# The head of a fused convolution, scan and attention kernel: order of the weights, depth of the convolution's pipeline, places for two buffers

## The chip, the cores and the metric

The kernel runs on one core of a Trainium2 chip. The core has a matrix engine (TensorE, PE in the profile), a vector engine (VectorE, DVE), a scalar engine (ScalarE, ACT), a general engine (GpSimd, POOL) and SyncE (SP), which here only issues transfers. Each runs its own list of instructions in order and waits on semaphores for the others. The metric is the time of one execution on the device in microseconds (us); lower is better.

## The reference, cut to what matters

The input `x` is (4, 64, 64, 96): four images. Layer 0 is a binarised Mamba-like block with four scan directions, layer 1 a linear attention and a quantised feed-forward. What bears on this case is the start of layer 0:

```python
xz = bilinear(x, W_in, s_in, b_in)            # sign(x) @ (s * sign(W - mean(W))).T + b
xp, z = jnp.split(xz, 2, axis=-1)             # 192 channels each
t = bq_quad(xc + move0_b)                     # the sign of xp, as channels by 64x64
t = conv3x3(t, mean|conv_W| * sign(conv_W))   # 192 -> 192 channels
t = prelu(t + conv_b + rp_b0) + rp_b1 + xc
xconv = jax.nn.silu(t)                        # called u in the kernel
x_hwwh = jnp.stack([x_flat, x_tr], axis=1)    # by rows and by columns
xs = jnp.concatenate([x_hwwh, jnp.flip(x_hwwh, axis=-1)], axis=1)   # four directions
x_dbl = bilinear(xin, Wl, sl, bl)             # per direction: 6 dt rows, 16 B, 16 C
dts = bilinear(dts_r, Wd, sd, bd)             # -> 192 step sizes per position
# selective scan over 4096 positions, 192 channels x 16 states, for each direction:
#   h = exp(dt * A) * h + dt * u * B;   y = sum(h * C) + D * u
# then LayerNorm, gate with silu(z), output projection, and layer 1
```

## The kernel before

The scans of the four images are one long loop of 1536 pieces (image, direction, chunk of 1024 positions, group of 32 channels, quarter of the states), which needs in each piece one product on POOL, one exponential on ACT, one scan on DVE, and a product on DVE or POOL. What the images need ahead of their scans (the prologue) runs beside the scans of the image before. Only the first image has nothing to run beside: its prologue is the **head** of the program. There the prologue (`first`, with `alone` true) and the preparation of all weights (`made`) are two generators; each `yield` hands over to the other, so the order of instructions on each engine is the order in which they take turns.

```python
made, first = c.weights(), prologue(c, 0, c.xts)
lanes = [made, first]
next(made)
for _ in range(6):
    next(first)
while (0, 1) not in c.ready:
    interleave(lanes)          # one step of each
    c.later.tick()
assert made not in lanes
scans = Scans(c)
```

`c.later` holds stores back: `store(dst, src, after=2)` is issued on SP's queue two ticks later, so that SP, which runs in order, need not wait for the data.

The prologue transposes the image (`xps`), takes its signs (`xsT`) and a copy with bias (`xb`), projects it (`ix`, `iz`: PSUM tags `y0` and `y1`; their signs `tp` and `sz` by ACT), and runs the convolution in 16 parts of 96 channels by 512 positions:

```python
for n, part in enumerate(parts + [None]):
    if part:
        h, q = part
        ps = c.p.dA.tile([128, CH], F32, ...)[0:96, 0:512]      # alone
    for s in range(4 if alone else 5):
        # four of the 15 taps of this part:  matmul(ps, w, tp)
        if alone and ahead:                     # project ahead, 12 parts of 16
            if s == 0:
                next(ahead[0])                  # matmuls ix, iz
            elif s == 2:
                next(ahead.pop(0), None)        # ACT: tp, sz
        if prev:                                # the part before
            ph, pq, pz, v, r, pn = prev
            if s == 0:                          # alone
                c.vec.scalar_tensor_tensor(pz, pz, S_X, v, ALU.mult, ALU.add)
                c.vec.scalar_tensor_tensor(pz, r, oma, pz, ALU.mult, ALU.add)
            elif s == 1:
                sign(ph, pq, pz)                # ACT sg, three stores into xg
                nc.scalar.activation(e, pz, AF.Exp, scale=-1.0)
            elif s == 2:
                nc.scalar.activation(e, e, AF.Ln, bias=1.0)
                nc.scalar.activation(e, e, AF.Exp, scale=-1.0)
            elif s == 3:
                c.vec.tensor_tensor(u, pz, e, ALU.mult)
                c.later.store(c.ud[b][ph][...], u)
                by_columns(ph, pq, u)           # POOL copies u turned into ut; utd <- ut
        yield
    if part:
        nc.vector.tensor_scalar(v, ps, acs, acb, ALU.mult, ALU.add)
        nc.scalar.activation(r, ps, AF.Relu, scale=csc, bias=cbias)
        pz = bank("cz" + nm, n % 2)
        nc.tensor.matmul(pz, winT, xsT)
        prev = (h, q, pz, v, r, nm)
        yield
```

(Cut: the branches for the other images, and arguments.) `sg`, `e`, `u`, `v`, `r`, `xb` are tiles of pool `f`, which has 8 buffers taken in turn. `ut` has a pool of its own, beside the convolution's tiles; the pool of the rows, opened next, takes over that memory.

The rows stage turns `xg` into rows (`xr`, twelve copies by ACT and DVE in turn), multiplies with the weights of two directions (`acc`), and writes B, C (`tbc`, stored to `bcd`) and the signs for dt (`sgn`, stored to `sgd`), in two halves. Each of `xa`, `xb`, `acc` is a PSUM bank of two in turn: `bank(f"xa{o}{n}", n % 2)`. `sgd` comes back as `g` and is turned into `gT`.

Then `Scans.start` loads the first columns of u and the first B (`bc`), computes the first step sizes, and sends them through a copying transfer to the scan's tiles (`dl_s`):

```python
w = [p.w.tile([128, CH], F32, name=f"w_s{x}", tag="w") for x in range(8)]
t, d2, us = w[4:6], w[6], w[2:4]
nc.sync.dma_start(v[0], ud[0:128, 0:16])                 # us, from utd
for q in range(NQ):
    self.load_bc(0, self.bt, 0, 0, 0, q)                 # four of 512 KB
for x in range(2):
    nc.sync.dma_start(v[1][64 * x : 64 * x + 64, 0:8], ud[128:DN, 8 * x : 8 * x + 8])
...
r = p.dl.tile([128, CH], F32, name=f"dl{x}_s{n}", tag=f"dl{x}")
nc.sync.dma_start(r, w[x][32 * n : 32 * n + 32].unsqueeze(1).to_broadcast([32, 4, CH]))
```

Of the kernel before, what the change touches and what calls it, by code (L numbers as in the profile page):

```python
# [25 lines left out]
CH = 1024  # L26
# [27 lines left out]
def hybrid_kernel(ctx: ExitStack, tc: tile.TileContext, a: dict, out: bass.AP):  # L54
# [108 lines left out]
    def weights():  # L163
# [110 lines left out]
        part = temp("part", [96, 2, 2])  # L274
        for i, cut in enumerate(cuts):
            nc.scalar.activation(cwA.rearrange("p t d -> p (t d)")[:, cut], cfa[i], AF.Sign, saturate=False)
            nc.scalar.activation(cwB[:, lines[i]], cfb[i], AF.Sign, saturate=False)
            for h in range(2):
                nc.vector.tensor_reduce(part[:, h, i : i + 1], cwn[h][i], AX.X, ALU.add, apply_absolute_value=True)
        nc.vector.tensor_tensor(csc, part[:, :, 0], part[:, :, 1], ALU.add)  # L280
        nc.vector.tensor_scalar(csc, csc, 1.0 / (9 * DN), None, ALU.mult)
        yield

        nc.vector.tensor_tensor(cbias, pv[:, :, CONV_B], pv[:, :, RP0], ALU.add)
        nc.vector.tensor_tensor(acs, pv[:, :, PRELU], csc, ALU.mult)
        nc.vector.tensor_tensor(acb, pv[:, :, PRELU], cbias, ALU.mult)
        nc.vector.tensor_tensor(acb, acb, pv[:, :, B_X], ALU.add)
        nc.vector.tensor_tensor(acb, acb, pv[:, :, RP1], ALU.add)
        nc.vector.tensor_scalar(oma, pv[:, :, PRELU], -1.0, 1.0, ALU.mult, ALU.add)
        for h in range(2):  # L290
            nc.gpsimd.tensor_scalar(omad[:, h], i96, oma[:, h : h + 1], None, ALU.mult)
        yield
# [5 lines left out]
        for o in range(2):  # L298
            m = negmean(f"wlm{o}", wl[o], DN)
            sw = temp(f"wls{o}", [128, DN], BF16)  # L300
            nc.scalar.activation(sw, wl[o], AF.Sign, bias=m)
            we = temp(f"wle{o}", [128, 4, 128], BF16)
            nc.gpsimd.memset(we, 0.0)
            for kk in range(2):
                rows = slice(64 * kk, 64 * kk + 64)
                for x, pair in enumerate(kinds[kk]):
                    for half, j in enumerate(pair):
                        if j is not None:
                            to, src = we[rows, x, 64 * half : 64 * half + 64], sw[rows, 64 * j : 64 * j + 64]
                            if o:  # L310
                                to = we[rows, x, half::2]
                            else:
                                to, src = to.rearrange("p (e i) -> p i e", e=2), src.rearrange("p (i e) -> p i e", e=2)
                            nc.gpsimd.tensor_copy(to, src)
            yield
            transposed(wR[:, o].rearrange("p x m -> p (x m)"), [we[:, x, :] for x in range(4)])
            yield

# [133 lines left out]
def run(c):  # L452

    made, first = c.weights(), prologue(c, 0, c.xts)
    lanes = [made, first]
    next(made)
    for _ in range(6):
        next(first)
    while (0, 1) not in c.ready:
        interleave(lanes)  # L460
        c.later.tick()
    assert made not in lanes
    scans = Scans(c)
    ends = [Epilogue(c, b, scans) for b in range(NB)]

    def back():

        yield from first
        yield from prologue(c, 1)
        for b in range(NB):  # L470
            while not scans.done(b, 2):
                yield
            yield from turn(c, b)
            if b + 2 < NB:
                yield from prologue(c, b + 2)
            e = ends[b]
            e.open()
            yield from e.sums(e.lane)
            if b + 1 < NB:
                yield from e.middle()  # L480
                yield from e.last(e.lane)
                e.close()

    behind = back()
    scans.run(behind)


    def drain(lanes):
        while lanes:
            interleave(lanes)  # L490
            c.later.tick()
        c.later.flush()

    e = ends[-1]
    e.alone = True
    more = [e.spare_lane(x) for x in range(2)]
    drain([behind] + [e.sums(ln) for ln in more])
    more.append(e.fourth_lane())
    drain([e.middle()])
    drain([e.last(ln) for ln in [e.lane] + more])  # L500
    e.close()


def prologue(c, b, xts=None):
# [11 lines left out]
    with tc.tile_pool(name=f"xg_{b}", bufs=1) as xgp:  # L516
# [3 lines left out]
        with tc.tile_pool(name=f"cv_{b}", bufs=1) as cvp:  # L520
# [123 lines left out]
            utp = sub.enter_context(tc.tile_pool(name=f"ut_{b}", bufs=1))  # L644
            uts = {}

            def by_columns(h, q, u):


                per = 2 if alone and h else 4  # L650
                if q % per == 0:
                    uts[h] = utp.tile([96, IW, 8 * per], F32, name=f"ut{h}{q}_{b}", tag=f"ut{h if alone else 0}")
                ut, at = uts[h], 8 * (q % per)
                dst, src = ut[:, :, at : at + 8], u.rearrange("p (h w) -> p w h", w=IW)
                (nc.gpsimd.tensor_copy if alone else nc.scalar.copy)(dst, src)
                if q % per == per - 1:
                    rows = slice(8 * (q + 1 - per), 8 * q + 8)
                    c.later.store(c.utd[b][h].rearrange("p (w h) -> p w h", h=IH)[:, :, rows], ut, after=1)

            def sign(h, q, pz):  # L660
# [5 lines left out]
                for m in range(3):  # L666
                    g0 = 64 * (m // 2) + 32 * h
                    c.later.store(xgw[g0 : g0 + 32, m % 2, 128 * q : 128 * q + 128], sg[m::3, :])

            for n, part in enumerate(parts + [None]):  # L670
                if part:
                    h, q = part
                    nm = f"{h}{q}"
                    if alone:
                        ps = c.p.dA.tile([128, CH], F32, name=f"cv{nm}_{b}", tag="dA")[0:96, 0:512]
                    else:
                        ps = bank("cv" + nm, 0)[0:96]
                for s in range(4 if alone else 5):
                    if part:
                        per = 4 if alone else 3  # L680
                        for tp, w, dy, dx in taps[per * s : per * s + per]:
# [4 lines left out]
                    if alone and ahead:  # L686
                        if s == 0:
                            next(ahead[0])
                        elif s == 2:
                            next(ahead.pop(0), None)  # L690
# [3 lines left out]
                    if prev:  # L694
                        ph, pq, pz, v, r, pn = prev
                        if s == 0:
                            if alone:
                                c.vec.scalar_tensor_tensor(pz, pz, pv[:, ph, S_X : S_X + 1], v, ALU.mult, ALU.add)
                                c.vec.scalar_tensor_tensor(pz, r, c.oma[:, one(ph)], pz, ALU.mult, ALU.add)
                            else:  # L700
                                nc.scalar.mul(pz, pz, pv[:, ph, S_X : S_X + 1])
                        elif s == 1 and not alone:
# [3 lines left out]
                        elif s == (1 if alone else 2):  # L706
# [4 lines left out]
                        elif s == (2 if alone else 3):  # L711
                            nc.scalar.activation(e, e, AF.Ln, bias=1.0)
                            nc.scalar.activation(e, e, AF.Exp, scale=-1.0)
                        elif s == (3 if alone else 4):
# [4 lines left out]
                            if alone:  # L719
                                by_columns(*turned)  # L720
                                turned = None
                    yield
                if part:
                    v, r = f32("v" + nm)[0:96], f32("r" + nm)[0:96]
                    if alone:
                        nc.vector.tensor_scalar(v, ps, c.acs[:, one(h)], c.acb[:, one(h)], ALU.mult, ALU.add)
                    else:
                        nc.scalar.activation(v, ps, AF.Identity, scale=c.acs[:, one(h)], bias=c.acb[:, one(h)])
                    nc.scalar.activation(r, ps, AF.Relu, scale=c.csc[:, one(h)], bias=c.cbias[:, one(h)])  # L729
                    pz = bank("cz" + nm, n % 2 if alone else 1)[0:96]  # L730
# [12 lines left out]
        with tc.tile_pool(name=f"rw_{b}", bufs=1) as rw:  # L743
# [7 lines left out]
            gw = g2.bitcast(F32)  # L751
            for o in (1, 0):
# [10 lines left out]
                for n in range(13):  # L763
# [3 lines left out]
                    if n < 8:  # L767
                        ps = bank(f"xa{o}{n}", n % 2)
# [3 lines left out]
                    elif n < 12:  # L772
                        ps = bank(f"xb{o}{n}", n % 2)
# [9 lines left out]
                for gh in range(2):  # L783
                    groups = slice(32 * gh, 32 * gh + 32)
                    prev = None
                    for n in range(5):
# [9 lines left out]
                        if n < 4:  # L796
                            acc = prev = bank(f"acc{o}{gh}{n}", n % 2)
# [36 lines left out]
                for x, k in enumerate((o, o + 2)):  # L834
                    nc.sync.dma_start(gw[:, x, 16:64], c.sgd[b][k].rearrange("(p f) -> p f", p=128))
                    yield
# [412 lines left out]
class Scans:  # L1249
# [232 lines left out]

    def start(self):
# [3 lines left out]
        w = [p.w.tile([128, CH], F32, name=f"w_s{x}", tag="w") for x in range(8)]  # L1487
        t, d2, us = w[4:6], w[6], w[2:4]
        ud = c.utd[0].rearrange("h p (n l) -> (h p) n l", l=IW)
        v = [u.rearrange("p (n l) -> p n l", l=IW) for u in us]  # L1490
        nc.sync.dma_start(v[0], ud[0:128, 0:16])
        for q in range(NQ):
            self.load_bc(0, self.bt, 0, 0, 0, q)
        for x in range(2):
            nc.sync.dma_start(v[1][64 * x : 64 * x + 64, 0:8], ud[128:DN, 8 * x : 8 * x + 8])
# [170 lines left out]
```

## Time and profile before

| what | us |
|---|---|
| median of three runs (5474.62 to 5479.99) | 5479.21 |
| profiled execution, span | 5482.3 |
| DVE busy | 5016.3 (91%) |
| POOL busy | 4938.7 (90%) |
| ACT busy | 3615.3 (66%) |
| PE busy | 3415.9 (62%) |
| POOL's first product of the scans starts at | 235.32 |
| first tap of the convolution, last `v`, first `xr` start at | 56.21, 170.94, 188.25 |

How to read it: a view by stretch gives each engine's busy time between two moments; a group line names the source line (L423 is a helper that many operations go through, so the tile names tell them apart), the engine, the operation and the tiles, out first. A wait line reads "this engine, before these instructions, waited for that engine or transfer", with the total, the number and the longest. Idle time of an engine that is not the bottleneck costs nothing. SPq is SyncE's queue: how long SP was held by the issue of a transfer, not how long the transfer took.

### The profile page before, as it was taken

The numbers are of one execution on the slowest core, as the hardware profiler recorded it, in microseconds if no ns is written. First come the engines' busy times: TensorE is split into PE (matmuls) and PEld (weight loads), VectorE is DVE, ScalarE is ACT, GpSimd is POOL, SyncE is SP. The second block draws the span as 40 slices with busy tenths as digits, with TensorE's granted clock in tenths as the row PEclk, the third lists the DMA queues.
The fourth block names the chain that finished last, engine by engine and source line by source line (L and its number), as shares of the span: only waits on it lengthen the run. The fifth ranks groups of instructions, "written<-read, shape, count | busy, mean of one in ns | idle before, by whom it ended". The sixth has DMA issues, their size and how long they took to land. (4 is left out here: it accounts for less than half of the span.)

```text
span 5482.3 us, 62080 instructions
## 1 busy us (share of the span) xinstructions
PE 3415.9 (62%) x20083; PEld 1355.4 (25%) x20083; DVE 5016.3 (91%) x3171; ACT 3615.3 (66%) x5648; POOL 4938.7 (90%) x2245
## 2 busy tenths in 40 slices
PE   6456665467656776657764676664676664444577
PEld 3222222122222222222222222221232221111233
DVE  4499999899999999999999999999999999999994
ACT  4467777687766667778777666776666775555554
POOL 2399999899999999999999999999999999999990
PEclk7666776678766777767886787766787666666777
DMA  4565666767666666576665665667666565665652
GB/s 82 128 211 171 207 207 199 228 213 213 195 200 201 189 208 204 196 244 213 217 199 181 216 198 186 216 192 225 217 218 187 189 204 194 195 211 194 212 175 62
DMA packets 624219, 1069.06 MB, mean 195 GB/s; under 512 B 237307, under 2 KB 355092, under 8 KB 622100
## 3 DMA queue, kind: packets, MB, share of 16 engines
q1 hardware_dynamic: 623236, 1065.07, 62.2%
q8 instruction: 157, 2.57, 0.2%
q14 instruction: 170, 1.39, 0.1%
q10 hardware_dynamic: 656, 0.02, 0.0%
HBM read 830.01 MB, written 228.56 MB: 193 GB/s over the span
## 5 line engine op out<-in xcount | busy, mean ns | idle before, releaser
L423 POOL TENSOR_TENSOR w<-dl,bc 128x1024 f32<-128x1024 f32 x1524 | 3550.0, 2355 | 88.0 <-PE yp L1462 52.8
L1389 ACT ACTIVATE dA<-dl,anm 128x1024 f32<-128x1024 f32 x1524 | 1701.1, 1116 | 486.0 <-DVE w L423 284.5
L423 DVE TENSOR_TENSOR_SCAN dA<-dA,cy,w 128x1024 f32<-128x1024 f32 x725 | 1698.6, 2343 | 107.8 <-ACT dA L1389 94.2
L423 POOL TENSOR_TENSOR w<-h,bc 128x1024 f32<-128x1024 f32 x570 | 1341.4, 2353 | 127.8 <-DVE h L423 113.6
L1462 PE MATMUL yp<-w,sum 128*32 128x256 f32 x12288 | 1254.7, 505 | 323.8 <-ACT pd L1343 235.0
L423 DVE TENSOR_TENSOR w<-dA,bc 128x1024 f32<-128x1024 f32 x966 | 1183.1, 1225 | 65.4 <-DMA bc<-bcd 4.0
L423 DVE TENSOR_TENSOR_SCAN h<-dA,cy,w 128x1024 f32<-128x1024 f32 x427 | 999.2, 2340 | 17.4 <-ACT dA L1389 16.7
L1462 PEld LDWEIGHTS yp<-w,sum 128*32 128x32 f32 x12288 | 316.9, 127 | 1401.0 <-issue 731.4
L1431 ACT COPY cy<-dA 128x1 f32<-128x1 f32 x725 | 114.0, 157 | 753.2 <-DVE w L423 751.3
L423 DVE TENSOR_TENSOR_SCAN dA<-dA,w 128x1024 f32<-128x1024 f32 x241 | 550.2, 2283 | 34.7 <-ACT dA L1389 28.0
L1324 PE MATMUL dps<-gT,wdz 128*128 128x64 fp8e5 x1008 | 116.6, 316 | 399.9 <-ACT ys L1476 373.9
L423 DVE TENSOR_TENSOR_SCAN h<-dA,w 128x1024 f32<-128x1024 f32 x143 | 325.9, 2279 | 18.8 <-POOL w L423 16.1
L1337 PE MATMUL dps<-sp,ident 128*128 128x512 f32 x378 | 268.5, 799 | 96.2 <-ACT dps L1333 96.1
L1467 PE MATMUL yp<-ya,back 128*128 128x256 f32 x576 | 226.3, 511 | 0.0
L682 PE MATMUL cv<-tp,cwA 128*96 128x512 fp8e5 x576 | 197.9, 467 | 33.3 <-ACT r L729 30.9
L1324 PEld LDWEIGHTS <-wdz 128*128 128x128 fp8e5 x1008 | 95.6, 153 | 479.2 <-issue 451.7
L1324 PE MATMUL dps<-gT,wdy 128*128 128x64 fp8e5 x504 | 58.7, 318 | 221.0 <-ACT ys L1476 220.8
L1431 ACT COPY cy<-h 128x1 f32<-128x1 f32 x427 | 79.3, 186 | 133.5 <-DVE h L423 132.8
L994 PE MATMUL yc<-eys,mean 96*96 96x512 f32 x240 | 141.4, 744 | 29.5 <-DVE vks L423 14.4
L1329 ACT ACTIVATE pd<-dps,dbias,pvd 128x512 f32<-128x512 f32 x189 | 143.9, 761 | 20.8 <-PE dps L1324 20.5
L1467 PEld LDWEIGHTS yp<-ya,back 128*128 128x128 f32 x576 | 117.6, 236 | 119.9 <-issue 88.2
L1330 ACT ACTIVATE sp<-dps,dbias,pvd 128x512 f32<-128x512 f32 x189 | 144.8, 766 | 0.0
(363 smaller groups left out, 4457.2 us busy)
## 6 DMA issues: line engine op xcount, KB each, us to landing
dl<-dld SPq DMA_DIRECT2D x762, 512.0 KB
bc<-bcd SPq DMA_DIRECT2D x512, 512.0 KB
dld<-pd SPq DMA_DIRECT2D x126, 512.0 KB
yd<-ys SPq DMA_DIRECT2D x768, 64.0 KB
dld<-pd SPq DMA_DIRECT2D x126, 256.0 KB
ya<-yd SPq DMA_DIRECT2D x192, 128.0 KB
pu<-ud SPq DMA_DIRECT2D x32, 512.0 KB
pu<-utd SPq DMA_DIRECT2D x31, 512.0 KB
```

Source lines behind the costliest of these rows:

```text
L423: return getattr(self.eng, name)(out, *args, **kw)
L682: nc.tensor.matmul(ps, w[:, 96 * h : 96 * h + 96], tp[:, 8 * q + dy : 8 * q + dy + 8, dx : dx + IW], start=(w is taps[0][1]), stop=(w is t ...
L994: self.c.nc.tensor.matmul(ps, w, x, start=(i == 0), stop=(i == len(pairs) - 1))
L1324: nc.tensor.matmul(pv[:, s], wd[:, k, s], gT[:, :, c0 : c0 + 16], start=(s == 0), stop=(s == 7))
L1329: nc.scalar.activation(d[:, 0], ps, AF.Abs, scale=sc, bias=bi)
L1330: nc.scalar.activation(t, ps, AF.Relu, scale=sc, bias=bi)
L1337: nc.tensor.matmul(ps, c.ident, t, start=False, stop=True, skip_group_check=True)
L1389: c.nc.scalar.activation(t, self.dlt[i // NQ][0], AF.Exp, scale=c.anm[:, g, NQ * KORD[e] + q : NQ * KORD[e] + q + 1])
L1431: self.c.nc.scalar.copy(self.carries[g, q], h[:, CH - 1 : CH])
L1462: c.nc.tensor.matmul(y[32 * x : 32 * x + 32, g % 2, :], c.sum4, prod[:, 256 * x : 256 * x + 256], start=(q == 0), stop=(q == NQ - 1 and no ...
L1467: c.nc.tensor.matmul(y[:, g % 2, :], w, src, start=False, stop=(n == len(more) - 1))
```

## The change

The change touches only the head; it is for filling its engines better and for keeping transfers out of each other's way. It has six pieces. The weights take one step for every two of the image's steps, and the scales of the convolution (`csc`, `acs` and others) are made later in their order. The convolution of the first image becomes a pipeline of three parts: matmuls of part n, combination and signs of n-1, the end of the sigmoid and u of n-2. The turned u (`ut`) of the first image lies in tiles of the scans' pool `w`, two q per store instead of four for h=0, and the last store of each h is held until the convolution's other stores are issued. The signs of the first image are stored from GpSimd's queue at once instead of from SP's queue two ticks later. The rows of the first image use four PSUM banks (`b0`, `b1`, `y0`, `y1`) instead of two. The loads of the first B and u for the scans are issued right after the loads of `g`, ahead of `start`.

The diff, cut to its core ("# ..." marks cuts):

```diff
@@ weights
-        part = temp("part", [96, 2, 2])
         for i, cut in enumerate(cuts):
             nc.scalar.activation(cwA..., cfa[i], AF.Sign, saturate=False)
             nc.scalar.activation(cwB[:, lines[i]], cfb[i], AF.Sign, saturate=False)
-            for h in range(2):
-                nc.vector.tensor_reduce(part[:, h, i : i + 1], cwn[h][i], AX.X, ALU.add, apply_absolute_value=True)
-        # ... csc, cbias, acs, acb, oma, omad
+        yield
+        def scales():
+            # ... the same reductions, csc, cbias, acs, acb, oma, omad
@@ after the first of two transposes into wR
+            if o == 0:
+                scales()
+                yield
@@ run
+    scans = Scans(c)
+    c.loads_ahead = scans.first_loads
     # ...
+    next(made)
     while (0, 1) not in c.ready:
-        interleave(lanes)
+        interleave([first])
         c.later.tick()
+        if (0, 1) not in c.ready:
+            interleave(lanes)
+            c.later.tick()
@@ by_columns, sign
-                per = 2 if alone and h else 4
+                per = 2 if alone else 4
+                    if alone:
+                        ut = c.p.w.tile([128, CH], F32, name=f"ut{h}{q}_{b}", tag="w")[0:96]
+                    if alone and q == NQ8 - 1:
+                        held.append((dst, ut))
+                    else:
+                        c.later.store(dst, ut, after=1)
-                    c.later.store(xgw[g0 : g0 + 32, m % 2, 128 * q : 128 * q + 128], sg[m::3, :])
+                    if alone:
+                        nc.gpsimd.dma_start(dst, sg[m::3, :])
+                    else:
+                        c.later.store(dst, sg[m::3, :])
@@ alone_parts, for the first image
+                for n, part in enumerate(parts + [None, None]):
+                    for s in range(4):
+                        # ... four taps of part n
+                        if s == 0:
+                            # ... next(ahead[0]);  two scalar_tensor_tensor of part n-1
+                        elif s == 1 and end:
+                            nc.scalar.activation(e, e, AF.Ln, bias=1.0)          # part n-2
+                            nc.scalar.activation(e, e, AF.Exp, scale=-1.0)
+                        elif s == 2:
+                            # ... next(ahead.pop(0), None);  then of part n-1:
+                                sign(mh, mq, pz)
+                                nc.scalar.activation(e2, pz, AF.Exp, scale=-1.0)
+                        elif s == 3 and end:
+                            c.vec.tensor_tensor(u, epz, e, ALU.mult)             # part n-2
+                            c.later.store(c.ud[b][eh][:, 512 * eq : 512 * eq + 512], u)
+                            by_columns(eh, eq, u)
+                        yield
+                    # ... v, r, cz of part n as before
+            if alone:
+                yield from alone_parts()
+                c.later.flush()
+                for dst, src in held:
+                    nc.sync.dma_start(dst, src)
@@ rows
+            def row_bank(nm, j, fast):
+                if fast and j % 4 > 1:
+                    return c.p.ps.tile([128, 512], F32, name=f"{nm}_{b}", tag=f"y{j % 2}")
+                return bank(nm, j % 2)
-                        ps = bank(f"xa{o}{n}", n % 2)
+                        ps = row_bank(f"xa{o}{n}", n, fast)
                  # ... the same for xb and acc
                     nc.sync.dma_start(gw[:, x, 16:64], c.sgd[b][k].rearrange("(p f) -> p f", p=128))
+                    if fast and x:
+                        c.loads_ahead()
@@ Scans
+    def first_loads(self):
+        # ... the four load_bc and the loads of us, out of start(), in tiles of their own
```

## The prediction

> **What bounds the kernel now.** I read four views, in this order. First the page's forty slices, to see whether any part of the program looks different from the rest:
>
> ```profile
> DVE  4499999899999999999999999999999999999994
> ACT  4467777687766667778777666776666775555554
> POOL 2399999899999999999999999999999999999990
> ```
>
> One slice is 137 us. From the third slice on, DVE and POOL are both at 90%: the scan loop is bound by these two, and every instruction it holds is needed. Only the first two slices, the head, have room. Second, the busy times by stretch of the head (columns: the stretch, its length, then busy us and count of PE, PEld, DVE, ACT, POOL, then the granted clock, DMA share, GB/s):
>
> ```profile
> 90.00:148.00 58.00, 40.88 (x146) 19.78 (x145) 23.02 (x32) 38.13 (x60) 8.36 (x8) 0.88 0.52 95
> 148.00:177.00 29.00, 15.47 (x49) 7.43 (x48) 14.65 (x21) 15.55 (x25) 5.50 (x6) 0.74 0.41 69
> 177.00:188.30 11.30, 1.05 (x8) 0.93 (x9) 0.00 (x0) 0.05 (x1) 0.82 (x2) 0.50 0.71 100
> 188.30:212.00 23.70, 13.27 (x144) 11.08 (x143) 10.53 (x14) 9.63 (x14) 0.20 (x2) 0.50 0.16 36
> 212.00:235.40 23.40, 4.95 (x52) 4.61 (x52) 4.18 (x7) 10.70 (x18) 0.08 (x1) 0.57 0.73 223
> 235.40:300.00 64.60, 29.01 (x250) 13.28 (x250) 49.72 (x28) 40.25 (x68) 62.55 (x28) 0.60 0.55 169
> ```
>
> In no stretch before 235.4 is an engine full; after it POOL is busy 62.55 of 64.6 us. So POOL's first scan product, at 235.32 us, is the end of the head, and what is cut from the head comes off the whole, nearly one for one. Third, the waits of the first 300 us:
>
> ```profile
> POOL w L423 <- DMA dl_s<-w_s: 46.8, 1, 46.8
> DVE u L423 <- ACT e L713: 54.5, 15, 4.6
> ACT r L729 <- DVE v L726: 29.7, 16, 4.3
> PE xa L760 <- DMA xg<-sg: 15.3, 1, 15.3
> ACT xr L765 <- DMA utd<-ut: 12.3, 1, 12.3
> ```
>
> DVE waits 54.5 us for the sigmoid (`e`), ACT 29.7 us for `v`: a ring in which each waits for the other, once per part of the convolution. The last two lines are one gap, between convolution and rows. Fourth, its cause in SP's own timeline:
>
> ```profile
> 172.16 0.58 SPq L442 DMA_DIRECT2D utd<-ut  x1
> 172.84 6.02 SPq L442 DMA_DIRECT2D ud<-u  x1
> 178.95 1.77 SPq L442 DMA_DIRECT2D xg<-sg  x3
> 180.81 0.59 SPq L442 DMA_DIRECT2D utd<-ut  x1
> 181.50 4.97 SPq L442 DMA_DIRECT2D ud<-u  x1
> ```
>
> Whatever is issued after a `utd` store holds SP 5 to 6 us: that store consists of 6144 short runs. The signs, ready at 174.1, leave at 178.95; the first `xr` starts at 188.25, when the last `utd` store has left the memory that `xr` takes over.
>
> **What the Trainium skill says.** (1) "TensorE: Matmul & The Clock Gate", Part 1: the clock is halved when TensorE has idled and released by sustained work. The trace agrees: 0.50 in the sparse stretch 188 to 212, 0.88 in the dense one 90 to 148; taps follow each other at 0.22 us when fast and 0.43 when slow. (2) "PSUM — Partial Sum Buffer", PSUM bank collisions: two engines must not touch one bank at once, reads included. The trace agrees: `r` starts 0.83 us after `v`, at its end, though both only read `cv`. (3) "SBUF — State Buffer", Who interferes with whom: a DMA issued by GpSimd can starve while DVE holds the shared port. No run here shows it yet; in the convolution `v`, `cz` and `u` have an operand in PSUM, so I expect little of it.
>
> **The change part by part.**
>
> *Weights at half pace.* Before, the scale reductions sit ahead of the first `xb` on DVE and wait for the `cw_n` load (to 20.5 us), so the third transpose starts at 24.46. Afterwards they stand behind six `xb`, but the second weight transpose and GpSimd's clearing of `tp` stand behind them. Following DVE's order with the trace's durations, DVE waits for `wl` until about 21.5, then mean, ACT's signs, GpSimd's 12 copies (3.82) and the transposes bring `wR` to 27.5; two `xb` and the reductions (4.0 plus 1.1 of small ones) go to 34.7; two `xb`, the second mean, signs and copies (2.3) to 39.5; clearing `xg` and `tp` (0.95, 1.95) to 42.5. Before, it was 42.6: nothing gained there. The four projections that follow took from 42.3 to 55.3 with `wdz` casts in between; ACT's own work is two times 3.87 plus 1.63 of signs, 9.4 us, so convolution starts near 52 instead of 56.2. But its first part now has three groups of eight transposes on a slow TensorE, and I carry only 2 us of that gain to its end.
>
> *Three parts deep.* Before, one part costs 7.33 us with a projection (`v` at 82.06 and 148.01, nine periods) and 5.7 without (153.7 to 170.94, three). ACT works 38.13 us for eight parts in 90 to 148: 4.8 each. Its sum from starts in the timeline agrees: `sg` 0.49, `e` 0.48, `tp` 0.66 or 1.55, `sz`, Ln, Exp, `r` 0.66 each. The rest is the ring v, two `cz`, sg, e, Ln, Exp, u, v. With Ln, Exp and u of the part before moved into the time in which DVE makes `cz`, ACT no longer waits. TensorE needs 18 matmuls at 0.22, 3.9 us when fast; DVE 0.8+0.76+0.75+0.69=3.0; GpSimd one copy of 1.06 and three DMA issues, which I put at about 1 us each (an estimate from SP's 0.59 for the same issue), 4.1. ACT stays the longest: I take 5.1 with small waits. Parts without projection: GpSimd's 4.1 is longest, I take 4.3.
> Parts 0 to 3 also carry the weights: per part about 3 us of DVE casts and some 4 us of GpSimd; I take 6.5 each, against 26.6/3=8.9 before. Sum from first to last `v`: before 107.8; after 3x6.5+8x5.1+4x4.3=77.5, plus 2 for the remaining small weights on DVE and 5 for `sg` waiting for the store of an older `u` (pool `f` has 8 buffers, five are used per part; a `ud` store lands some 8 us after its `u` when it stands behind a `utd` store, and `sg` wants the buffer 1.75 parts, about 9 us, later): 84.5. **23 us saved.**
>
> *u by columns in the scans' tiles, signs from GpSimd's queue.* The signs no longer stand behind the `utd` store, and the last two `utd` stores are held until the end, in memory that the rows do not use. Before, last `v` to first `xr`: 170.94 to 188.25, 17.3 us. After: v to sg 3.4, three issues 3, landing 2 (the two loads of `g`, issued from 213.10, let TensorE start at 214.75), `xa` 0.6: 9 to 10. **7.5 saved.** Price: eight `utd` stores of 6144 runs instead of six, on SP, off the path while SP has room.
>
> *Four banks.* A pair of row copies took 1.37 us (189.06 to 190.43) with its matmuls 1.01 of it; afterwards 1.0, so six pairs save 2.2. A pair of `acc` took 2.84 with 1.67 of DVE; afterwards 2.0 by TensorE at half clock: 1.5 over the first half. The second half waits for the `bcd` store (4.0 us, unchanged), but four accumulators are ready by then: 1.2. **5 saved.**
>
> *First loads ahead.* `dl_s` was issued at 225.75 and landed at 233.9: 8 us, behind 3.25 MB of `bc`, `w_s` and `pu` issued from 218.2. Now 2.75 MB of that go at about 214.6 of the old clock and are through by some 224.5 at 290 GB/s (the rate of 220 to 240). `dl_s`, 1 MB, then needs 4 to 5 us instead of 8. **3.5 saved.**
>
> Sum: 2+23+7.5+5+3.5 = 41 us. The instructions of the scan loop are the same in the same order on every engine. 5479 less 41 is 5438; I add 2 for waits that I have not foreseen: **5440 us**.
>
> **Rivals.**
> *A: GpSimd's queue becomes the bound.* It now has `ut`, the weights' clears and copies and the signs' issues in order. For: GpSimd has 4 us of weights per early part, and TensorE's order puts the transposes between taps. Against: it is busy only 8.36 of 58 us in 90 to 148. At 2 us per issue a part costs over 7 us, the convolution gains nothing, and the time is about 5462.
> *B: the ring only moves.* TensorE stays at half clock (18x0.43=7.7 per part) or `sg` waits for `ud` stores each time. For: both occur in the trace (half clock at 131 to 137; 1.9 us of `sg` waiting for `ud`). Against: less waiting makes TensorE denser and keeps its clock up. It would leave some 10 of the 23: 5453.
> *C: the loop gives it back.* The head's gain is lost because the first scans wait for `dl` loads. Against: after 235 GpSimd idles only 2 us. It would add 3 to 5 us.
> *D: better than I think.* If parts 0 to 3 run at 5 us and `sg` never waits, the convolution saves 33: 5430.
>
> **Range and chances.** The spread is that of the convolution, 10 to 33 us, and a few us in each other term: 5425 to 5460. Faster by 2% needs 110 us, half the head; slower needs 110 us more; neither is in sight.
>
> **What would show it.** First scan product of GpSimd near 195 us instead of 235.3; `v` to `v` near 5.1 with and 4.3 without projection; ACT over 90% busy there; last `v` to first `xr` under 11 us; four copies of rows between PE waits; `dl_s` landing within 5 us of issue; busy times after the head unchanged. Wrong would make it: a DMA issue of 2 us on POOL, TensorE at 0.5 in the convolution, or `sg` waiting for `ud` in every part.

## The result and the profile after

The changed kernel takes 5450.02 us (median of four runs, 5449.25 to 5452.13), the kernel before on the same chip 5478.45 (four runs, 5474.62 to 5479.99). The ratio is 0.995, with a 95% interval of 0.9933 to 0.9967: a gain of 28 us, within the 2% band. The profiled spans are 5482.3 and 5450.3 us.

The starts of the same events in both traces (us) show where the time was gained:

| event | before | after | earlier by |
|---|---|---|---|
| first tap of the convolution | 56.2 | 48.0 | 8.2 |
| first `v` | 63.2 | 58.7 | 4.4 |
| fifth `v` | 96.6 | 93.5 | 3.1 |
| last `v` | 170.9 | 159.1 | 11.9 |
| first `xr` | 188.25 | 167.9 | 20.4 |
| issue of the last `sgd` store over | 212.1 | 186.9 | 25.2 |
| first product of the scans on POOL | 235.3 | 212.7 | 22.6 |

The head became 22.6 us shorter. The difference of the two profiles at the starts of the scans stays at 22 to 23 us up to scan 448 and goes up to 28.6 by scan 512; a second profile of the kernel before, told of below, shows how much of such a jump is not the change's.

The stretches of the head, in the changed kernel (columns as in the prediction's view: stretch, length, busy us and count of PE, PEld, DVE, ACT, POOL, then granted clock, DMA share, GB/s):

```profile
90.00:148.00 58.00, 39.48 (x176) 20.60 (x177) 28.91 (x58) 37.87 (x62) 22.86 (x36) 0.82 0.57 69
148.00:165.00 17.00, 10.11 (x46) 5.28 (x43) 11.01 (x15) 11.86 (x21) 8.15 (x14) 0.95 0.81 127
168.00:185.00 17.00, 9.30 (x147) 8.18 (x145) 9.97 (x14) 8.48 (x13) 0.20 (x3) 0.80 0.70 85
```

In the first line ACT is busy 37.87 of 58 us, hardly different from the 38.13 before: the convolution has not become dense. The third line is the rows stage: TensorE's clock there is 0.80, where it was 0.50.

The waits of the first 300 us say why (engine, waited for: us in total, times, longest):

```profile
POOL w L428 <- DMA dl_s<-w_s: 44.5, 1, 44.5
...
ACT r L739 <- DVE v L738: 26.2, 8, 6.8
...
DVE v L738 <- DMA ud<-u: 9.9, 1, 9.9
ACT e L726 <- DMA ud<-u: 9.8, 2, 8.1
...
DVE u L428 <- ACT e L718: 4.7, 9, 1.5
```

The wait that the three-deep order was made to remove is gone: DVE waits 4.7 us for the sigmoid `e` in place of 54.5. But ACT's wait for `v` is nearly as long as before (26.2 in place of 29.7), in half as many pieces, and two long waits for `ud<-u` are new, one for each of the two engines: a buffer of pool `f` whose store has not been carried out. SP's own timeline holds the reason (start, how long SP was held):

```profile
102.38 0.58 SPq L447 DMA_DIRECT2D utd<-ut  x1
103.01 5.30 SPq L391 DMA_DIRECT2D sbR<-in_sl_bc  x1
...
112.76 17.36 SPq L397 DMA_DIRECT2D anm<-in_al  x24
130.22 1.52 SPq L447 DMA_DIRECT2D ud<-u  x3
131.84 0.61 SPq L447 DMA_DIRECT2D utd<-ut  x1
132.54 5.23 SPq L447 DMA_DIRECT2D ud<-u  x1
```

From 103 to 130 us SP issues the 36 small loads of the weights' last step (12 `sbR`, 24 `anm`), at first held by a `utd` store. Three finished `u` wait behind them until 130.22. In the kernel before the same loads stood between 69.9 and 92.4, and no engine waited for a transfer of u or of the signs from 66 to 98 us there; the half pace has moved them:

```profile
76.17 16.25 SPq L392 DMA_DIRECT2D anm<-in_al  x24
92.52 0.56 SPq L442 DMA_DIRECT2D ud<-u  x1
```

DVE in the changed kernel, from 133 us on:

```profile
133.34 0.81 DVE L738 TENSOR_SCALAR v<-cv,acs,acb 96x512 f32<-96x512 f32 x1 [9.90 <-DMA ud<-u]
...
140.31 0.69 DVE L428 TENSOR_TENSOR u<-cz,e 96x512 f32<-96x512 f32 x1 [4.44 <-DMA ud<-u]
...
147.19 0.81 DVE L738 TENSOR_SCALAR v<-cv,acs,acb 96x512 f32<-96x512 f32 x1 [2.77 <-DMA xg<-sg]
```

The bracket is the idle time ahead of the instruction and what ended it. The second wait, at 140.31, has another cause: the `ud` store at 132.54 was held for 5.23 us by the `utd` store ahead of it. The third, at 147.19, ends with a store of signs, which GpSimd had issued.

From `v` to `v`, the fifteen intervals of the changed kernel are 7.1, 10.0, 10.4, 7.2 | 6.7, 4.2, 3.9, 4.9, 5.8 | 14.3, 7.6, 6.3 | 4.4, 3.8, 3.7 us. The second and the fourth group sum to what the prediction has for them, within 1 us; the first is that of the weights, the third that of the three waits just shown.

The two other steps that GpSimd and the early loads bear on:

```profile
99.80 1.47 POOL L689 DMA_DIRECT2D xg<-sg  x3 [5.60 <-ACT sg L681]
```

Three issues of the signs hold POOL 1.47 us, 0.49 each.

```profile
192.03 0.75 SPq L1563 DMA_DIRECT2D w_u<-utd  x1
...
201.77 0.69 DVE L428 TENSOR_TENSOR w_s<-w_s,w_u 128x512 f32<-128x512 f32 x1 [2.51 <-DMA w_u<-utd]
...
203.09 1.31 SPq L1611 DMA_DIRECT2D dl_s<-w_s  x2
...
212.71 2.34 POOL L428 TENSOR_TENSOR w<-dl_s,bc 128x1024 f32<-128x1024 f32 x1 [44.51 <-DMA dl_s<-w_s]
```

The first piece of u, issued behind the four of B and C, now ends last ahead of `w_s`: DVE waits 2.51 us for it. And the step sizes, whose way to the scans' tiles starts at 203.09, release POOL 9.6 us later, the same as before (225.75 to 235.32), though the loads that I had blamed for this were through. The stretches around it (the last column is GB/s of all transfers):

```profile
192.00:202.00 10.00, 4.32 (x41) 4.05 (x38) 0.92 (x2) 8.08 (x14) 0.00 (x0) 0.50 0.98 295
203.00:204.00 1.00, 0.00 (x0) 0.00 (x0) 0.96 (x4) 0.00 (x0) 0.00 (x0) 0.50 0.00 0
204.00:207.00 3.00, 0.00 (x0) 0.00 (x0) 1.20 (x2) 0.00 (x0) 0.00 (x0) 0.50 0.84 101
```

Nothing was moving when `dl_s` was issued, and then all transfers together moved 101 GB/s, where the loads of B and u had moved 295.

### The profile page after: what moved, and what is told of

Same layout as the page of the kernel before. It is cut to its first block, busy times and chain, and to the rows that moved or that the text cites. A ratio compares the mean times of both kernels' runs of the same rounds, so it can differ in the third digit from the quotient of the medians.

```text
span 5450.3 us, 62113 instructions
## 1 busy us (share of the span) xinstructions
PE 3400.9 (62%) x20083; PEld 1346.5 (25%) x20083; DVE 5015.9 (92%) x3171; ACT 3614.6 (66%) x5648; POOL 4961.9 (91%) x2293
## 5 line engine op out<-in xcount | busy, mean ns | idle before, releaser
L428 DVE TENSOR_TENSOR_SCAN h<-dA,cy,w 128x1024 f32<-128x1024 f32 x427 | 999.1, 2340 | 16.6 <-ACT dA L1461 15.8
L428 DVE TENSOR_TENSOR_SCAN h<-dA,w 128x1024 f32<-128x1024 f32 x143 | 325.9, 2279 | 21.9 <-POOL w L428 10.9
L761 PE MATMUL cv<-tp,cwA 128*96 128x512 fp8e5 x432 | 150.5, 466 | 29.2 <-ACT r L793 26.8
L1539 PEld LDWEIGHTS yp<-ya,back 128*128 128x128 f32 x576 | 118.4, 238 | 121.9 <-issue 93.5
```

The lines of the kernel that those rows point to most:

```text
L428: return getattr(self.eng, name)(out, *args, **kw)
L761: nc.tensor.matmul(ps, w[:, 96 * h : 96 * h + 96], tp[:, 8 * q + dy : 8 * q + dy + 8, dx : dx + IW], start=(w is taps[0][1]), stop=(w is t ...
L1539: c.nc.tensor.matmul(y[:, g % 2, :], w, src, start=False, stop=(n == len(more) - 1))
```

## The experiments

All but the last change the new kernel, and nothing but its head; each was timed beside the kernel before, whose median was 5480.9 us beside the first four, 5477.7 beside the next four and 5477.1 beside the last three. The first four ask what kept the convolution and the first loads back.

**The small weight loads early.** The 36 loads read inputs only; they are issued right after the second transpose into `wR`.

```diff
+        # after the second transpose into wR
+        for k in range(NK):   # three loads into sbR each
+        for g in range(NG):   # four loads into anm each
@@ last step of the weights
-        # the same 36 loads
```

> The changed kernel, with the 36 small weight loads (sbR, anm) of the weights' last step issued on SP right after the second transpose into wR, when SP is idle. Theory 1 (these loads hold SP from 103 to 130 us in the middle of the convolution, the ud stores stand behind them, and pool f runs out of buffers): the standstill of DVE from 123 to 133 us is gone, first to last v falls from 100.4 to about 90 us, GpSimd's first scan product comes near 203 instead of 212.7, the time is near 5440. Theory 2 (SP is full with the utd stores anyway): the standstill only moves, first to last v stays above 97 us, the time is within 3 us of 5450.

Measured: 5445.61 us (5444.72 to 5448.71), ratio 0.994 (0.9925 to 0.9955). First to last `v` 91.2 us in place of 100.3, first product at 203.7 in place of 212.7. The interval of 14.3 is gone (6.3 in its place); intervals of 7.0, 6.3 and 6.5 stay. So the 36 loads, moved by the half pace, cost 9 us of the head; the position of the product is met, the time is within 6 us of it.

**u ahead of B and C.** `first_loads` issues the three loads of u first.

```diff
     def first_loads(self):
-        for q in range(NQ):
-            self.load_bc(0, self.bt, 0, 0, 0, q)
         # ... three loads of us
+        for q in range(NQ):
+            self.load_bc(0, self.bt, 0, 0, 0, q)
```

> The changed kernel, with the loads of u ahead of the four loads of bc instead of behind them. Theory 1 (u waits behind 2 MB of bc: the first product of du started 2.5 us after its other operand): first product at 210.2 instead of 212.7 us, time near 5447.5. Theory 2 (the transfer dl_s is what ends last and waits for the whole of the earlier loads, in whatever order): dl_s lands at the same moment, the time stays at 5450.

Measured: 5446.09 us (5442.42 to 5452.44), ratio 0.9941 (0.9926 to 0.9956); first product at 209.9, 2.8 us earlier. From the end of the last `sgd` issue to the first product it is 23.3 us in place of 25.8 (23.2 before the change). The order of these seven loads is what the early issue had lost.

**u in tiles of its own.** `u` leaves pool `f` and takes halves of a tile of pool `pd`, two parts to a tile.

```diff
-                            u = f32("u" + en)[0:96]
+                            if eh == 0:
+                                uu = c.p.pd.tile([128, 2, 512], F32, name=f"uu{en}_{b}", tag="pd")
+                            u = uu[0:96, eh]
```

> The changed kernel, with u of the first image in tiles of pool pd (four halves in turn, idle until the scans) instead of pool f. Theory 1 (sg, e and v wait for ud stores only because u shares the 8 buffers of f): no wait for ud<-u is left in the convolution, first to last v falls from 100.4 to about 85 us, but SP's backlog of stores then ends no earlier than about 160 us, so that first product is near 200 to 203 us and the time near 5438. Theory 2 (the convolution is held by SP through other buffers too, ut or sz in pool w): a wait of the same length appears at another tile and the time stays within 3 us of 5450.

Measured: 5459.41 us (5456.21 to 5465.6), ratio 0.9964 (0.9952 to 0.9977); first product at 213.7, 1.0 us later than in the changed kernel, first to last `v` 102.6. The head is no faster, and the gain of the median is 7 us smaller (the two intervals overlap). My expectation fell. The several waits became one interval of 24.0 us between two `v`:

```profile
111.36 16.25 SPq L397 DMA_DIRECT2D anm<-in_al  x24
127.72 1.52 SPq L447 DMA_DIRECT2D ud<-uu  x3
130.22 0.69 DVE L428 TENSOR_TENSOR uu<-cz,e 96x512 f32<-96x512 f32 x1 [19.80 <-DMA ud<-uu]
```

The same 36 loads hold SP; `uu` itself is now the ring that runs out, and DVE stands still until its stores have left, 19.80 us. More places for u don't help while the queue that empties them is held. After the standstill the intervals are 5.9, 3.9, 3.9, 4.9, 3.8, 3.5, 3.8: no wait of 4 to 7 us is left.

**Turned u in long runs.** The `utd` stores keep their number and bytes, but each writes 96 runs of 4 KB instead of 6144 short ones. This kernel leaves the order by columns out of the stored u.

```diff
+                    if alone:
+                        at = 512 * (q + 1 - per)
+                        dst, ut = c.utd[b][h][:, at : at + CH], ut.rearrange("p w h -> p (w h)")
```

> The changed kernel, with the turned u of the first image stored as 96 runs of 4 KB per store instead of 6144 runs of 64 bytes (it goes to other places of utd, so the columns' order of u is not what the reference asks; bytes and number of stores are the same). Theory 1 (the short runs hold SP 5 to 6 us per store): SP's issues behind utd fall below 1 us, the waits of 4.4 and 2.8 us for ud and xg at 136 and 144 us vanish, the standstill at 123 to 133 stays since it comes from the weight loads; first product near 205 us, time near 5443. Theory 2 (DMA traffic in general holds SP): SP is held as before and the time stays at 5450.

Measured: 5443.42 us (5437.29 to 5446.17), ratio 0.9933 (0.9919 to 0.9948). First to last `v` 89.4, last `v` to first `xr` 7.0, first product at 199.4. A pair of stores in SP's timeline:

```profile
139.10 0.30 SPq L447 DMA_DIRECT2D utd<-ut  x1
139.49 0.38 SPq L447 DMA_DIRECT2D ud<-u  x1
```

Against 0.61 and 5.23 us in the changed kernel (131.84 and 132.54): the holding of SP belongs to the many short runs, not to the bytes. The waits of 4.44 and 2.77 us are gone too. One interval of 10.2 us is left in this kernel: ACT waits 7.09 us for a `ud` store while SP is held by the 36 loads (the 24 `anm` take 16.58 us from 105.26).

The next four undo one part of the change each. Two pieces were not undone alone: the depth of three, and the new place of `ut` with its held last stores.

**The weights at full pace.** The later place of the scales stays.

```diff
-        interleave([first])
+        interleave(lanes)
         c.later.tick()
-        if (0, 1) not in c.ready:
-            interleave(lanes)
-            c.later.tick()
```

> Part (1) of the change undone alone: the weights again take a step with every step of the image, all else as in the changed kernel. Theory 1 (the half pace moves the 36 small weight loads from before 93 us to 103-130 us, where they hold the stores of u): the loads are issued near 70-95, no standstill of 10 us in the convolution near 123, but the first parts of the convolution, which then share GpSimd, ScalarE and TensorE with twice the weight work, take longer (parts 0 to 4 some 40 us in place of 34.8); first to last v 95-102 against 100.3, first product of the scans 208-214 against 212.7, time 5446-5452 against 5450. Rival (the half pace is what the depth of three needs; the standstill comes from the u stores alone and stays): first to last v over 103, first product over 215, time over 5453.

Measured: 5445.73 us (5441.94 to 5452.63), ratio 0.9947 (0.9932 to 0.9962); first product at 201.7, 11 us earlier than with the half pace. No 10 us standstill, as expected; but the first parts are not slower, they are much faster: 6.7, 3.9, 3.9, 4.8 between the first five `v` in place of 7.1, 10.0, 10.4, 7.2. That part of my expectation was wrong. The first tap comes at 60.6 instead of 48.0, since more of the weights is done ahead of it, but the fifth `v` is at 89.3 instead of 93.5, and the last at 147.8 instead of 159.1 (77.8 us from first to last, where I had expected 95 to 102). The 12.6 us by which the half pace starts the convolution earlier are more than given back by the fifth `v`.

**Two banks for the rows.**

```diff
-                if fast and j % 4 > 1:
+                if False:
```

> Part (4) undone alone: the rows' products rotate over two banks again. Theory 1 (the step of 5 us for the four banks): from the first xr to the last row on its way 23-24 us in place of 19, everything before it unchanged, first product near 217.5 against 212.7, time 5454-5456. Rival (the rows follow the row loads and the SyncE issues, banks count for nothing): first product within 1 us of 212.7.

Measured: 5460.69 us (5455.76 to 5463.69), ratio 0.997 (0.9958 to 0.9981); first product at 216.8, 4.1 us later. First `xr` to the end of the last `tbc` is 21.9 us, as before the change, against 17.1. The rows stage of this kernel:

```profile
168.00:185.00 17.00, 11.07 (x122) 9.53 (x120) 7.30 (x10) 6.08 (x10) 0.00 (x0) 0.50 0.65 77
```

TensorE does 122 matmuls in 11.07 us at clock 0.50, against 147 in 9.30 at 0.80 with four banks. In the ten traces with four banks the clock of the rows stage (17.2 us from the first `xr`) is 0.70 to 0.80, in the three with two (22 us from it) 0.50. So the banks act twice: copies overlap with matmuls, and TensorE, which waits less, gets more of its clock. The Trainium skill, "TensorE: Matmul & The Clock Gate", Part 1, describes the second, and the two numbers agree with it.

**The signs from SP.**

```diff
-                    if alone:
-                        nc.gpsimd.dma_start(dst, sg[m::3, :])
-                    else:
-                        c.later.store(dst, sg[m::3, :])
+                    c.later.store(dst, sg[m::3, :])
```

> The GpSimd part of (3) undone alone: the signs of the convolution go out from the SyncE queue, after the step, as before the change; u by columns stays. Theory 1 (signs from SyncE are kept back by the u stores' short runs and by the weights' loads): first to last v unchanged or 2 us shorter (GpSimd no longer waits for the signs, 64 us of waits in all, so its copies of u and weights come earlier), last v to first xr 12-18 us in place of 8.8, first product 216-222 against 212.7, time 5453-5460. Rival (GpSimd standing in line for the signs costs as much as it brings): first product within 2 us of 212.7 or earlier.

Measured: 5466.23 us (5459.73 to 5474.41), ratio 0.9981 (0.9974 to 0.9989); first product at 221.7, 9.0 us later than in the changed kernel. The position of the first product is as expected, the way to it is not, and the time is 6 us over it: first to last `v`, which I thought would stay or shorten, became 6.1 us longer (106.4), last `v` to first `xr` only 2.5 us (11.3). SP after the 36 loads, where it makes up for what it was kept from:

```profile
108.17 16.30 SPq L397 DMA_DIRECT2D anm<-in_al  x24
...
125.23 1.84 SPq L447 DMA_DIRECT2D xg<-sg  x3
...
127.79 1.77 SPq L447 DMA_DIRECT2D xg<-sg  x3
```

With the signs, too, behind the loads, one interval of 23.4 us appears; in it DVE waits 19.15 us for a `ud` store. The queue of GpSimd keeps them out of this.

**The first loads back in `start`.** In the old place and the old order.

```diff
     # rows: after the second load of g
-                    if fast and x:
-                        c.loads_ahead()
     # start
+        self.first_loads()      # u's first piece, four of B and C, the rest of u
```

> Part (5) undone alone: the scans' first loads are issued after the last row again, in the old order, u's first piece ahead of the four of b and c. Theory 1 (loads issued ahead bring nothing because the wait that ends last is that of u behind b and c, and of the step row's 8 us of its own): last row to first product 22-25 us against 25.8, first product 209-213 against 212.7, time within 3 us of 5450. Rival (my step as predicted: loads ahead save 3.5): last row to first product 29, first product near 216, time 5454.

Measured: 5449.96 us (5442.32 to 5450.91), ratio 0.995 (0.9935 to 0.9965); first product at 209.4, 3.3 us earlier than in the changed kernel, as expected. Of these 3.3, 1.0 arises before the loads are issued; from the last `sgd` issue to the first product it is 23.5 us in place of 25.8. The early issue, in the order that it has, costs rather than saves; against the early issue in the better order (23.3) the old place loses only 0.2.

The last three put together what the others had shown, and look at the kernel before once more.

**All three mended.** Small loads early, u ahead of B and C, u in pool `pd`, at half pace.

> The changed kernel with three things moved at once: the 36 small weight loads early, the first pieces of u ahead of those of b and c, and u of the first image in the pool of pairs. Theory 1 (the 24 us standstill of u in the pool of pairs came from those 36 loads holding SyncE, and the waits of 4 to 7 us that stay without them come from the short runs of the u stores, which four places of u can bridge): no wait of DVE on a u store over 3 us, first to last v 84-88 in place of 91.2, last v to first product 51, first product 194-198, time 5434-5440. Rival (u in the pool of pairs waits for its own stores at the rate at which the short runs leave, so the deeper ring only puts the waits off): first to last v 91-95, first product 200-204, time 5441-5447.

Measured: 5438.43 us (5433.67 to 5441.65), ratio 0.9928 (0.9916 to 0.9941). First to last `v` 83.8, first product at 193.6. DVE's waits for u stores are one of 0.67 us, and one of 3.74 after the last `v`. The pool that had made a standstill of 19.80 us while SP was held removes the remaining waits once SP is free.

**The same with the weights at full pace.** The edit of the full pace and those of u ahead of B and C and of pool `pd`; the small loads are then early of themselves.

> The changed kernel with the weights at full pace again, the first pieces of u ahead of those of b and c, and u of the first image in the pool of pairs. Theory 1 (at full pace the weights' loads are through before the convolution, and the waits of 9.0, 8.7 and 6.8 us between v that remain are the short runs of the u stores): first to last v 66-72 in place of 77.8, first product 191-196, time 5433-5440. Rival (the stores' rate bounds, whatever the ring): first to last v 76-80, first product 198-200, time 5440-5446.

Measured: 5428.39 us (5424.35 to 5435.64), ratio 0.9914 (0.9901 to 0.9928), the fastest of all, and faster than I expected. First to last `v` 67.0, first product at 187.1.

```profile
51.91 16.26 SPq L397 DMA_DIRECT2D anm<-in_al  x24
```

```profile
80.00:120.00 40.00, 36.07 (x160) 19.16 (x158) 26.00 (x37) 39.55 (x66) 22.89 (x36) 1.00 0.61 99
```

The first line is SP's: the loads are through at 68.2, ahead of the first `v` (69.1). The second, a stretch of the convolution, is what the depth of three was for: ACT busy 39.55 of 40 us, TensorE's clock 1.00.

**The kernel before again.**

> The kernel before once more, for a second profile of it. Of the 32 us between the two profiled spans 22.6 lie ahead of the first product, and the rest appears between scans 448 and 512. Theory 1 (the rest belongs to that one profile of the kernel before and not to the change): the second profile has its first product within 1 us of 235.3, but its scans from 512 on lie 3-6 us ahead of the first profile's, and its span is 5475-5480. Rival (the loop itself runs faster by some 6 us after the change): the second profile repeats the first within 1 us throughout.

Measured: 5476.1 us (5466.66 to 5489.0), ratio 1.0 (0.9991 to 1.0009). The first product is at 235.0, as in the first profile (235.3); its scans from 512 on start 4.7 us ahead of those of the first profile, and its span is 5474.6. Two profiles of one and the same kernel thus differ by a jump of 3.0 us between scans 448 and 512 (1.7 to 4.7), against 5.5 in the comparison with the changed kernel. Against the second profile the changed kernel's first product is 22.3 us earlier and its span 24.3 us shorter. So most of what I wanted to explain is no work of the change, and the rest can't be told from such noise: the 22.6 us of the head lie inside the measured interval (0.33% to 0.67% of 5478, 18 to 37 us). Nothing shows that the loop became faster.

All runs on one table, gain of the head (235.3 less the first product) and gain of the median against the kernel before beside it:

| kernel | head | median |
|---|---|---|
| the signs from SP | 13.6 | 11.5 |
| two banks | 18.5 | 17.0 |
| u in tiles of its own | 21.6 | 21.5 |
| the changed kernel | 22.6 | 28.4 |
| u ahead of B and C | 25.4 | 34.8 |
| first loads back in `start` | 25.9 | 27.7 |
| small loads early | 31.6 | 35.3 |
| full pace | 33.6 | 32.0 |
| turned u in long runs | 35.9 | 37.5 |
| all three mended | 41.7 | 38.7 |
| the same at full pace | 48.2 | 48.7 |

## Why the prediction was right, and where it was not

The time lay 10 us above the number and within the range. The frame of the prediction held: the head's gain comes off the whole one for one, as the table shows over 13 to 48 us, within 3 us in all but three rows and 10 in the worst. But the sum of 41 us was 22.6 in the trace. The median gained 5.8 us more than that, which no step explains, so in part the time came near 5440 by luck. The terms of the sum went as follows.

| step | predicted | measured |
|---|---|---|
| weights at half pace, to the first `v` | 2 | 4.4 |
| three parts deep, first to last `v` | 23 | 7.5 |
| u by columns, signs from GpSimd, last `v` to first `xr` | 7.5 | 8.5 |
| four banks, first `xr` to last `sgd` issue | 5 | 4.8 |
| first loads ahead, to the first product | 3.5 | -2.6 |
| sum | 41 | 22.6 |

*Weights at half pace.* Right in sign: the convolution starts at 48.0, earlier than my 52. The step failed by where it stopped. I followed DVE's order up to the first `v` and did not follow SP's, in which the half pace moved the 36 loads; I had counted "2 for the remaining small weights on DVE" and nothing for SP. Undone alone, the half pace is worth minus 11 us; moving only the loads brings back 9. But it is not the loads alone: with the loads early and the deeper ring, full pace is still 6.5 us ahead (first product at 187.1 against 193.6), 5.4 of it by the fifth `v`.

*Three parts deep* is the term that was mis-sized, 7.5 for 23. The mechanism was right: in the free intervals, five in the middle and three at the end, the sum was 25.5 and 11.9 us against 25.5 and 12.9 predicted. That the five agree to a tenth is luck, since they run from 3.9 to 6.7. And the three at the end are not bound by GpSimd, as I had it:

```profile
151.50:159.10 7.60, 7.11 (x32) 3.93 (x32) 5.98 (x10) 5.47 (x10) 4.36 (x7) 1.00 0.92 103
```

TensorE is busy 7.11 of 7.60 us there and GpSimd 4.36. Two assumptions of the term fell. "I take 6.5 each" for parts 0 to 3: the four intervals took 34.7 us against 24.6 in my sum. In the full-pace kernel, where the first tap waits until more of the weights are done, the same four took 19.3. And of the 5 us put by for waits on older u stores: the three intervals from the standstill on took 28.2 us against 14.5. Moving the loads takes 9 us of it, the deeper ring with them another 7.4 (91.2 to 83.8). Together the two misses are 10.1 + 13.7, less 1.0 gained at the end and less the 7 us I had put by: 15.8, the 23 less 7.5 but for rounding.

*Signs and turned u.* Right as a whole (how the 8.5 us divide between the signs and the place of `ut` is not shown; the signs put back on SP cost 2.5 of them), and cheaper than thought: 0.49 us for an issue on POOL against my estimate of 1. The Trainium skill's "SBUF — State Buffer", Who interferes with whom, had been the reason to watch for issues that starve behind DVE; none shows in these issues, while DVE is busy half of the time.

*Four banks.* Right in size, for a reason that I had half: the sum took TensorE at half clock, and it got 0.80.

*First loads ahead.* Wrong in sign. I had put the 8 us of `dl_s`, from its issue to its first use by ACT, down to the 3.25 MB ahead of it. With those loads through it still took 7.3 us (203.09 to 210.42), and 9.6 to POOL's first product, as before: the queue ahead of it was worth under 1 us. What the early order did was to let u's piece, which had been first, stand behind 2 MB of B and C. From the last `sgd` issue to the first product the change took 25.8 us, u ahead 23.3, the old place and order 23.5, the kernel before 23.2: the early place by itself brings 0.2 at most. Why `dl_s` takes so long isn't settled: it starts with nothing else moving and yet slowly, four loads of `bc` are issued 1.4 us after it and run beside it, and no run here sent it alone. In the fastest kernel, too, ACT could use it only 6.7 us after its issue (177.69 to 184.42).

*The rivals.* A (GpSimd the bound) did not come: POOL was busy 22.86 of 58 us. B is what happened, in its second half: u stores, though by SP's queue and not "each time"; its 5453 was nearer than my 5440. C did not show. D did not show in this kernel, but the one at full pace with `pd` and u ahead went beyond what D said: 67.0 us from first to last `v`, 41 less than before, where D had 33.

## What to carry to other kernels

When two streams of instructions are interleaved at another pace, follow the order of every queue, that of the engine that only issues transfers first of all: 36 small loads that kept no engine waiting where they stood cost 9 us once they stood ahead of the stores that free the buffers of a deeper pipeline. A deeper pipeline needs its buffers emptied, not just other or more of them: with the same pool `pd` the convolution was no faster while the queue was held (102.6 against 100.3 us) and faster once it was free (83.8 against 91.2). Where a transfer seems slow because of what is queued ahead of it, see whether it is any faster with the queue empty before counting on the gain.

## What was not expected of the hardware

A store of 6144 short runs takes SP 0.6 us itself but holds what SP issues next: 5.0 to 6.4 us in the convolution of the changed kernel; with the same bytes in 96 runs the next issue took 0.37 to 0.55. In the 3 us after `dl_s` was issued, with nothing moving before it, all transfers together moved 101 GB/s, where loads just before had moved 295. An issue of a 16 KB store of signs held POOL 0.49 us and, in threes behind one another, 1.8 us on SP (0.6 each). Two more PSUM banks raised TensorE's clock in a stage of small products from 0.50 to 0.80, and the convolution with hardly a wait in it ran at 1.00 (80 to 120 us of the fastest kernel), where in the changed kernel, with its waits, it was granted 0.82 (90 to 148).
